# Attention on one Trainium2 core: the row maxima moved from PSUM to SBUF, and two PSUM banks given to the common ring

## The chip, the core and the metric

The kernel runs as one program on one core of a Trainium2 chip. A core has five engines with queues of their own that work side by side: PE (TensorE, matrix products into PSUM), DVE (VectorE), ACT (ScalarE), POOL (GpSimd) and SP (SyncE, which here only issues DMAs). Each engine works through its own queue in order; semaphores make one wait for another. The metric is the device time of one execution in microseconds (us); lower is better.

## The reference

Three layers on one sequence of 512 tokens of 512 features, all in fp32: a cross attention to 8192 context tokens, a linear-attention stack of eight layers, and a small expert layer. Only the first is touched by the change. Cut to what matters:

```python
xn = layer_norm(x, gamma_x, beta_x)            # the context, 8192 tokens
ln = layer_norm(latents, gamma_l, beta_l)      # the 512 tokens
q = (ln @ Wq)                                  # 8 heads of 64
k_x, v_x = halves of xn @ Wkv;  k_x = rope_rotate_k(k_x)
k_l, v_l = halves of ln @ Wkv
k, v = concat of the context's and the tokens' own
sim = einsum('bhid,bhjd->bhij', q * d ** -0.5, k)
attn = softmax(sim, axis=-1)
out = einsum('bhij,bhjd->bhid', attn, v) @ Wo
```

There are 8192 + 512 = 8704 keys, that is 68 chunks of 128 keys.

## The kernel before, in words

The eight heads are taken as four pairs. A pair's 68 chunks are cut into units of at most 13 chunks; there are 24 units and 4 x 68 = 272 chunks of a pair of heads in all. The attention runs in steps of two chunks, 136 steps, and each step also carries a piece of the work that makes keys and values of a later block of the context (`keys_of`, `values_of`, L290 and L308) and of its normalization (L179, L92 to L104, L218).

For every chunk, PE multiplies keys by queries into two PSUM banks `pc`, one for each head, 128 keys by 512 queries (`score`, L477). ACT copies each into half of an SBUF tile `sc` of 128 x 1024 (L480), and DVE keeps a running elementwise maximum `mx` of the unit (L484, L486). At the end of a unit `maxima` transposes `mx` on PE (L495), reduces it on DVE to one maximum for each query (L498 to L501) and makes the factor `alpha` by which the earlier sums of this pair are shrunk (L504: two small SBUF tiles subtracted, 128 x 8). Then `maxima_rows` spreads the maxima over all partitions with eight PE transposes into `mbc` (L513), two PSUM banks wide, 128 x 1024.

`exponentials` works on the chunks of the unit while the next unit's scores are made: DVE subtracts `mbc` from `sc` in place (L541, one instruction for a chunk and both heads), ACT takes the exponential in place (L542), and POOL adds the tile into the unit's sum `es` (L550 for the first, L552 for the others; all of its operands lie in SBUF). `weigh` (L562) then multiplies it by the values on PE, and `sums` (L601) adds up `es` over the keys.

PE's queue is in the order in which the program is written (`manual_schedule`); the queues of DVE, ACT, POOL and SP are ordered by the framework's scheduler, with some hints (`issue_after`). POOL's queue in this part also holds the rotation of the keys (L315, L316), their DMAs to DRAM (L319), the scaling of the normalized features (L218) and small steps of the reciprocal roots (L92 to L104).

PSUM has eight banks. Here `ps_s`, a ring of five, serves `pc`, `pk`, `pv`, the transposes of `maxima` and others; `ps_m` holds one tile of two banks, first `means` (the column means of the weights, used once near 100 us by `column_means` and `centre_weights`), then every unit's `mbc`; `ps_o` holds one bank for the weighted values. The tiles `sc` come from `sp`, a ring of 19.

Of the kernel before, what the change touches and what calls it, by code (L numbers as in the profile page):

```python
# [8 lines left out]
F32 = mybir.dt.float32  # L9
I32 = mybir.dt.int32  # L10
AF = mybir.ActivationFunctionType
ALU = mybir.AluOpType
AX = mybir.AxisListType
PSUM = bass.MemoryType.PSUM
# [3 lines left out]
P = 128  # L18
D = 512
DC = D // P  # L20
T = 512
TT = T // P
# [17 lines left out]
C_GX, C_BX, C_GL, C_BL = 0, 4, 8, 12  # L40
# [15 lines left out]
def perceiver_kernel(  # L56
# [3 lines left out]
    nc = tc.nc  # L60

    def pool(name, bufs, space=None, stack=ctx, **kw):
        if space is not None:
            kw["space"] = space
        return stack.enter_context(tc.tile_pool(name=name, bufs=bufs, **kw))
# [9 lines left out]
    ident = cpool.tile([P, P], F32, name="ident")  # L75
    make_identity(nc, ident)
    x_sb = res.tile([P, TT, D], F32, name="x_sb")
    col = cpool.tile([P, NCOL], F32, name="col")
# [50 lines left out]
    def weights(p, src, name, queue=nc.sync):  # L129

        w = big_tile(p, name)[:, : DC * 512].rearrange("p (c f) -> p c f", c=DC)
        queue.dma_start(out=w, in_=src.rearrange("(c p) f -> p c f", p=P))
        return w


    xa = ExitStack()
# [4 lines left out]
    xpool = pool("xattn", 1, stack=xa)  # L141
    kvp = pool("x_kv", 16, stack=xa)
    ktp = pool("x_k", 4, stack=xa)
    sp = pool("x_s", 19, stack=xa)
    dram = pool("x_dram", 1, DRAM, stack=xa)
    ps_s = pool("ps_s", 5, PSUM, stack=xa)
    ps_m = pool("ps_m", 1, PSUM, stack=xa)
    ps_o = pool("ps_o", 1, PSUM, stack=xa)
    xa.enter_context(tc.manual_schedule(engines={nc.tensor.engine}))

# [6 lines left out]
    def bank(name, shape=None):  # L157
        return ps_s.tile(shape or [P, BLK], F32, tag="s", name=name)
# [71 lines left out]
    wkv = wpool.tile([P, 2, DC, D], F32, tag="wkv", name="wkv")  # L230
# [11 lines left out]
    g_d = xpool.tile([P, DC], F32, name="g_d")  # L242
# [26 lines left out]
    def column_means(i):  # L269

        for dc in range(DC):
            nc.tensor.matmul(
                means[:, i, :], g_d[:, dc : dc + 1].to_broadcast([P, P]), wkv[:, i, dc, :],
                start=(dc == 0), stop=(dc == DC - 1),
            )

    def centre_weights(i):

        for dc in range(DC):
            w = wkv[:, i, dc, :]  # L280
            nc.vector.scalar_tensor_tensor(
                w, w, col[:, C_GX + dc : C_GX + dc + 1], means[:, i, :], ALU.mult, ALU.subtract
            )

    def projected(ps, lhs, rhs):
# [10 lines left out]
    def keys_of(b, j):  # L296

        pk = bank("pk")
        projected(pk, lambda dc: wkv[:, 0, dc, j * P : (j + 1) * P], lambda dc: xT[b, dc])
        half = j % 2  # L300
        if half == 0:
            for c in ("cos0", "sin0", "sin1", "cos1"):
                part[c] = tmp.tile([P, BLK], F32, tag=c, name=c)
        if b == 0:
            nc.scalar.copy(part["cos" + str(half)], pk)
        else:
            for i, c in enumerate(("cos", "sin")):
                nc.vector.scalar_tensor_tensor(  # L308
                    part[c + str(half)], pk, bias[:, 0, j : j + 1], trigs[b][:, i, :], ALU.add, ALU.mult
                )  # L310
        if half == 0:
            return
        lo, hi = part["cos0"], part["cos1"]
        if b:
            nc.gpsimd.tensor_tensor(lo, lo, part["sin1"], ALU.subtract)  # L315
            nc.gpsimd.tensor_tensor(hi, hi, part["sin0"], ALU.add)  # L316
        k_dr[b, j // 2] = dram.tile([2, P, BLK], F32, name=f"k{b}_{j // 2}")
        for i, half_of in enumerate((lo, hi)):
            (nc.gpsimd if b > 1 else nc.sync).dma_start(out=k_dr[b, j // 2][i], in_=half_of)  # L319
# [98 lines left out]
    normalize_block(2)  # L418
    for j in range(DC):
        keys_of(0, j)  # L420
    means = ps_m.tile([P, 2, T], F32, tag="m", name="means")
    column_means(0)
    centre_weights(0)
    column_means(1)
    for j in range(DC):
        beta_of(1, j)
        values_of(0, j)
    centre_weights(1)


# [38 lines left out]
    scores, mx, mrow, alpha, mbc, es, po = {}, {}, {}, {}, {}, {}, {}  # L469
# [36 lines left out]

    def maxima_rows(u):

        mbc[u] = ps_m.tile([P, 2, T], F32, tag="m", name="mbc")
        m = mrow[units[u][0]]  # L510
        for c in range(2 * TT):
            h, qc = divmod(c, TT)
            nc.tensor.transpose(  # L513
                mbc[u][:, h, qc * P : (qc + 1) * P], m[:, c : c + 1].to_broadcast([P, P]), ident
            )

    def factor(u):

# [117 lines left out]
    for u, n in enumerate(size):  # L636
        at(end[u], maxima if end[u] in pieced else late_maxima, u)
        at(end[u] + 1, maxima_rows, u)
        if units[u][1]:
            at(end[u] + 1, factor, u)  # L640
            at(end[u] + (3 if n > 11 else 2), shrink, u)
        for b in range(units[u][1] // TT, (units[u][2] - 1) // TT + 1):
            c0, c1 = max(units[u][1], b * TT), min(units[u][2], (b + 1) * TT)
            at(
                max(-1, (end[u] * 2 + 1 - n + c0 - units[u][1]) // 2 - 2),
                load_keys, u, b, (c0 - b * TT) * P, (c1 - b * TT) * P,
            )
        span = size[u + 1] if u + 1 < len(size) else n
        first = last + 1 if u + 2 < len(size) else 0
        for i in range(n):  # L650
            d = end[u] + 1 + i * span // n // 2
            at(d, late_exponentials if d in end[-3:] else exponentials, u, i)
            last = max(d + 1, first)
            at(last, late_weigh if u == len(size) - 2 and last == end[-1] else weigh, u, i)
        at(last, sums, u)
        if u == last_of[units[u][0]] and u + 1 < len(size):
            at(last + 1, sums_by_query, u)
            at(last + 2, ones_over, u)

    rank = {maxima_rows: 0, factor: 3.5, maxima: 2, exponentials: 3, shrink: 4, ones_over: 4, weigh: 5, sums: 6, late_weigh: 6.5, late_maxima: 7, late_exponentials: 8}  # L660
    for d in range(min(todo), max(todo) + 1):
        behind[1] = behind[0]
        for s in steps[2 * d : 2 * d + 2] if d >= 0 else ():
            score(*s)
        whole = {maxima, maxima_rows, sums_by_query}
        halved[0] = not any(f in whole for f, a in todo.get(d, []))
        for f, a in sorted(todo.get(d, []), key=lambda e: rank.get(e[0], 1)):
            f(*a)
# [44 lines left out]
    with ExitStack() as s_:  # L713
# [608 lines left out]
        for o in (4, 5):  # L1322
            w = cpl.tile([P, DC, D], F32, tag=("curT", "cur")[o % 2], name=f"f2_{o}")
# [86 lines left out]
        for o in range(NO + 2):  # L1410
            if o < NO:
                inner(o)
            if o < 2:
                w = weights(big, f2[(6 + o) * 512 : (7 + o) * 512, :], f"f2_{6 + o}", nc.scalar)
# [79 lines left out]
```

## Time and profile before

| | |
|---|---|
| median of 3 runs | 2559.41 us (2559.37 to 2564.78) |
| the profiled execution's own time | 2560.21 us |
| its span, first to last instruction | 2558.4 us |
| share of the span: PE, DVE, POOL, ACT | 97%, 70%, 53%, 44% |
| attention steps, about 115 to 1185 us: busy PE, DVE, POOL, ACT | 1040.0, 824.2, 798.6, 605.0 us of 1070 |
| L541, `sc` minus `mbc`, 272 times | 318.8 us of DVE |
| L550 and L552, `es` sums, 23 and 222 times | 54.5 and 526.3 us of POOL |
| mean granted TensorE clock | 0.993 |

How to read it: the profile is of one execution. A row of a group gives the line of the kernel, the engine, the operation, what it writes and reads, shapes, count, then busy time in us and the mean of one in ns, then the idle time of the engine ahead of it and what ended that. An instruction's duration on DVE and POOL includes time in which it has begun and is held up by something that the rows do not name. The idle time of an engine that others do not wait for costs nothing.

### The profile page before, as it was taken

How to read it: one execution, taken by the hardware profiler on the slowest of the kernel's cores; microseconds unless marked ns; L12 is line 12 of the kernel's file. 1: busy time of each engine (PE TensorE's matmuls, PEld its weight loads, DVE VectorE, ACT ScalarE, POOL GpSimd, SP SyncE). 2: the span in 40 equal slices, each digit the busy share in tenths (PEclk: the TensorE clock that was granted, in tenths of full speed). 3: DMA queues.
4: the chain of work that ended last, by engine and by line, in shares of the span. 5: the costliest groups of instructions: out<-in, count | busy, mean ns of one | idle time of the engine just before them, and what ended most of it. 6: DMA issues, size and time to landing. Idle time of an engine off the chain costs nothing.

```text
span 2558.4 us, 33959 instructions
## 1 busy us (share of the span) xinstructions
PE 2493.9 (97%) x11712; PEld 1465.9 (57%) x11712; DVE 1783.0 (70%) x3722; ACT 1128.1 (44%) x2180; POOL 1364.9 (53%) x1496
## 2 busy tenths in 40 slices
PE   8999999999999999987999999999999999999998
PEld 4433333333333333333688686877868778687763
DVE  4467778777786777886765757667576676766764
ACT  2255555555555555663434415244152531525303
POOL 1157777777777876873153442535426353273512
PEclk9999999999999999998999999999999999999999
DMA  4222222222222221011523232232322323222235
GB/s 168 68 80 78 68 81 72 72 75 71 76 75 71 77 73 45 31 33 42 188 92 95 82 99 96 75 107 75 106 84 74 112 70 111 79 75 99 71 119 191
DMA packets 110019, 221.04 MB, mean 86 GB/s; under 512 B 7640, under 2 KB 11352, under 8 KB 109848
## 3 DMA queue, kind: packets, MB, share of 16 engines
q1 hardware_dynamic: 95336, 185.11, 21.6%
q10 hardware_dynamic: 8688, 15.94, 2.1%
q0 software_dynamic: 5824, 17.83, 1.9%
q8 instruction: 93, 1.52, 0.2%
q14 instruction: 78, 0.64, 0.1%
HBM read 195.78 MB, written 18.87 MB: 84 GB/s over the span
## 4 chain that ended last, share of the span: by engine, by line
PE 86%; DVE 6%; issue 2%; ACT 2%; POOL 2%; DMA 1%; ACTq 0%; DVEq 0%; POOLq 0%
PE pb L958 14%; PE ps L747 12%; PE pw L842 9%; PE pv L290 8%; PE pc L477 8%; PE pk L290 8%; PE po L562 7%; PE ps L842 6%; PE po L1121 4%; DVE sc L541 2%; POOL es L552 1%; PE pf L1051 1%; PE pt L1040 1%; PE mbc L513 1%; PE pmx L495 1%
## 5 line engine op out<-in xcount | busy, mean ns | idle before, releaser
L552 POOL TENSOR_TENSOR es<-es,sc 128x1024 f32<-128x1024 f32 x222 | 526.3, 2371 | 60.1 <-ACT sc L542 42.7
L542 ACT ACTIVATE sc<-sc 128x1024 f32<-128x1024 f32 x272 | 288.3, 1064 | 280.4 <-DVE sc L541 267.5
L486 DVE TENSOR_TENSOR mx<-pc,mx 128x512 f32<-128x512 f32 x448 | 281.5, 682 | 162.0 <-ACT sc L480 161.8
L480 ACT COPY sc<-pc 128x512 f32<-128x512 f32 x544 | 282.5, 599 | 92.6 <-PE pc L477 86.8
L541 DVE TENSOR_TENSOR sc<-sc,mbc 128x1024 f32<-128x1024 f32 x272 | 318.8, 1206 | 4.3 <-PE mbc L513 4.3
L477 PE MATMUL pc<-qT,kt 64*128 64x512 f32 x1088 | 283.6, 617 | 2.8 <-DVE sin L308 2.2
L562 PE MATMUL po<-sc,v 128*64 128x512 f32 x1088 | 262.8, 603 | 0.0
L290 PE MATMUL pk<-xn,wkv 128*64 128x512 f32 (+1 forms) x792 | 220.8, 603 | 5.0 <-DVE sin L308 2.6
L290 PE MATMUL pv<-wkv,xn 128*64 128x512 f32 (+1 forms) x816 | 220.8, 603 | 4.7 <-DVE sin L308 2.6
L477 PEld LDWEIGHTS pc<-qT,kt 64*128 64x128 f32 x1088 | 100.4, 186 | 181.2 <-issue 94.0
L1131 ACT ACTIVATE h<-h,col 128x256 f32<-128x256 f32 x192 | 103.7, 575 | 220.7 <-DVE h L891 151.1
L1015 ACT ACTIVATE g<-g 128x512 f32<-128x512 f32 x64 | 39.8, 628 | 345.5 <-DVE g L975 218.8
L842 PE MATMUL pw<-curT,cur 128*128 128x256 f32 (+1 forms) x896 | 177.2, 350 | 0.1
L924 POOL TENSOR_TENSOR sh<-h 128x128 f32<-128x128 f32 x120 | 80.8, 673 | 177.1 <-PE pb L958 172.0
L1098 POOL TENSOR_TENSOR y<-qf,y 128x512 f32<-128x512 f32 x32 | 44.5, 1390 | 244.7 <-DVE y L1097 232.1
L975 DVE TENSOR_TENSOR g<-g,pb 128x256 f32<-128x256 f32 x135 | 49.9, 416 | 158.7 <-PE pb L958 158.2
L842 PEld LDWEIGHTS pw<-curT,cur 128*128 128x128 f32 x896 | 150.2, 190 | 16.8 <-DVE curT L835 0.2
L829 POOL TENSOR_TENSOR cur<-w 128x256 f32<-128x256 f32 x128 | 93.2, 738 | 119.4 <-DVE g L1016 75.3
L290 PEld LDWEIGHTS pk<-xn,wkv 128*64 128x64 f32 (+1 forms) x792 | 72.5, 149 | 141.4 <-issue 111.2
L290 PEld LDWEIGHTS pv<-wkv,xn 128*64 128x64 f32 (+1 forms) x816 | 71.4, 147 | 142.4 <-issue 105.3
L562 PEld LDWEIGHTS po<-sc,v 128*64 128x64 f32 x1088 | 74.5, 138 | 133.5 <-issue 124.3
L958 PE MATMUL pb<-tw,sh 128*128 128x256 f32 x540 | 136.2, 379 | 0.0
(240 smaller groups left out, 4777.8 us busy)
## 6 DMA issues: line engine op xcount, KB each, us to landing
w<-in_wf SPq DMA_DIRECT2D x64, 1024.0 KB
cb<-in_cx SPq DMA_DIRECT2D x62, 256.0 KB
xn<-in_cxt SPq DMA_DIRECT2D x15, 1024.0 KB
k<-cos POOLq DMA_DIRECT2D x60, 256.0 KB, 2.6
kt<-k SPq DMA_DIRECT2D x108, 128.0 KB
row<-in_rows ACTq DMA_DIRECT2D x48, 256.0 KB
f<-in_f SPq DMA_DIRECT2D x10, 1024.0 KB
tg<-in_trig SPq DMA_DIRECT2D x16, 512.0 KB
```

Of the source, the lines that this page charges most:

```text
L290: nc.tensor.matmul(ps[o : o + n, :], lhs(dc)[:, o : o + n], rhs(dc), start=(dc == 0), stop=(dc == DC - 1))
L477: nc.tensor.matmul(pc[h], kt[u, b][hs, o : o + P], qT[hs, p, :], start=True, stop=True)
L480: copied[0] = nc.scalar.copy(sc[:, h, :], pc[h])
L486: behind[0] = nc.vector.tensor_tensor(mx[u][:, h, :], pc[h], mx[u][:, h, :], ALU.max)
L541: nc.vector.tensor_tensor(sc, sc, mbc[u], ALU.subtract)
L542: nc.scalar.activation(sc, sc, AF.Exp)
L552: summed[0] = nc.gpsimd.tensor_tensor(es[u], es[u], sc, ALU.add)
L562: nc.tensor.matmul(po[u][h * HD : (h + 1) * HD, :], v_sb[b, p][:, t * P + h * HD : t * P + (h + 1) * HD], scores[u, i][:, h, :], start=(i ...
L747: nc.tensor.matmul(ps[:, t0 : t0 + n], w[:, dc, c0 : c0 + P], xT[:, dc, t0 : t0 + n], start=(dc == 0), stop=(dc == DC - 1),)
L842: nc.tensor.matmul(ps, lhs[:, k], rhs[:, k], start=(k == 0), stop=(k == 1))
L958: nc.tensor.matmul(ps[i], lhs, rhs, start=(q == 0 and i in (1, 2, 6, 5, 4)), stop=(q == self.N - 1 and i in (1, 2, 7, 3, 4)),)
L1131: nc.scalar.activation(h, h, AF.Gelu_apprx_tanh, bias=col[:, c : c + 1])
```

## The change

`mbc` becomes an SBUF tile of 128 x 1024 from `xpool`, one buffer. In `maxima_rows` the eight transposes go, four for each head, into a bank `pm` of the common ring, and ACT copies each bank into its half of `mbc`. L541 is the same instruction, but reads its second operand from SBUF. The pool `ps_m` is gone, and the ring `ps_s` has seven banks instead of five; `means` becomes two banks of that ring. The ring `sp` of score tiles has 18 tiles instead of 19, which frees the room for `mbc`.

```diff
-    sp = pool("x_s", 19, stack=xa)
+    sp = pool("x_s", 18, stack=xa)
...
-    ps_s = pool("ps_s", 5, PSUM, stack=xa)
-    ps_m = pool("ps_m", 1, PSUM, stack=xa)
+    ps_s = pool("ps_s", 7, PSUM, stack=xa)
...
-                means[:, i, :], g_d[:, dc : dc + 1].to_broadcast([P, P]), wkv[:, i, dc, :],
+                means[i], g_d[:, dc : dc + 1].to_broadcast([P, P]), wkv[:, i, dc, :],
...
-                w, w, col[:, C_GX + dc : C_GX + dc + 1], means[:, i, :], ALU.mult, ALU.subtract
+                w, w, col[:, C_GX + dc : C_GX + dc + 1], means[i], ALU.mult, ALU.subtract
...
-    means = ps_m.tile([P, 2, T], F32, tag="m", name="means")
+    means = [bank("means") for i in range(2)]
...
-        mbc[u] = ps_m.tile([P, 2, T], F32, tag="m", name="mbc")
+        mbc[u] = xpool.tile([P, 2, T], F32, tag="mbc", name="mbc")
         m = mrow[units[u][0]]
-        for c in range(2 * TT):
-            h, qc = divmod(c, TT)
-            nc.tensor.transpose(
-                mbc[u][:, h, qc * P : (qc + 1) * P], m[:, c : c + 1].to_broadcast([P, P]), ident
-            )
+        for h in range(2):
+            pm = bank("pm")
+            for qc in range(TT):
+                c = h * TT + qc
+                nc.tensor.transpose(
+                    pm[:, qc * P : (qc + 1) * P], m[:, c : c + 1].to_broadcast([P, P]), ident
+                )
+            nc.scalar.copy(mbc[u][:, h, :], pm)
```

## The prediction

> **What bounds the kernel now.** The page comes first: who is busy, and where the time of the engines goes.
>
> ```profile
> PE 2493.9 (97%) x11712; PEld 1465.9 (57%) x11712; DVE 1783.0 (70%) x3722; ACT 1128.1 (44%) x2180; POOL 1364.9 (53%) x1496
> ...
> L552 POOL TENSOR_TENSOR es<-es,sc 128x1024 f32<-128x1024 f32 x222 | 526.3, 2371 | 60.1 <-ACT sc L542 42.7
> L542 ACT ACTIVATE sc<-sc 128x1024 f32<-128x1024 f32 x272 | 288.3, 1064 | 280.4 <-DVE sc L541 267.5
> ...
> L541 DVE TENSOR_TENSOR sc<-sc,mbc 128x1024 f32<-128x1024 f32 x272 | 318.8, 1206 | 4.3 <-PE mbc L513 4.3
> ```
>
> PE is the bound, and DVE's subtraction L541 has half of POOL's duration per tile. The whole-span shares hide the stage that is changed, so the next view cuts out the attention steps.
>
> ```profile
> 115.00:300.00 185.00, 180.58 (x795) 68.63 (x794) 132.23 (x185) 102.78 (x195) 124.45 (x115) 0.99 0.24 77
> ...
> 700.00:900.00 200.00, 195.88 (x909) 72.92 (x906) 153.90 (x217) 111.36 (x204) 155.62 (x128) 0.99 0.22 73
> ...
> 1100.00:1185.00 85.00, 69.00 (x344) 29.25 (x340) 71.10 (x93) 51.31 (x80) 64.24 (x27) 0.92 0.06 17
> sum 1070.00, PE 1040.01 PEld 394.85 DVE 824.23 ACT 604.99 POOL 798.63; mean PE 173.33 PEld 65.81 DVE 137.37 ACT 100.83 POOL 133.10
> ```
>
> The columns after the length are PE, PEld, DVE, ACT and POOL. In these 1070 us PE idles for 30, DVE for 246, POOL for 271. So at most 30 us can be won here while PE's work stays the same, and DVE and POOL, each near 75%, are close behind. The waits of PE say what a larger ring could win:
>
> ```profile
> PE mbc L513 <- DVE sc L541: 10.9, 3, 4.9
> ...
> PE means L272 <- DVE wkv L281: 2.8, 1, 2.8
> PE pk L290 <- DVE sin L308: 2.6, 1, 2.6
> ```
>
> PE waits 10.9 us for the old `mbc` to come free, with 7.9 more put down to its weight loads; the waits for a ring bank are 2 to 3 us each.
>
> The deciding view is another: what happens to a DVE instruction whose two inputs both lie in SBUF while POOL works. L541 is none now (its `mbc` is in PSUM), but L504 is one, on 8 elements, and L218 another.
>
> ```profile
> L541 DVE TENSOR_TENSOR sc<-sc,mbc x272: 1168/1210/1221, 120.3 to 1183.5; 128x1024 f32<-128x1024 f32 x136
> L504 DVE TENSOR_TENSOR alpha<-mrow x20: 159/468/4189, 267.3 to 1175.4; 128x8 f32<-128x8 f32 x20
> L218 POOL TENSOR_TENSOR xn<-xn,rbc x58: 1256/1277/1768, 64.5 to 997.4; 128x512 f32<-128x512 f32 x58
> ...
> L218 DVE TENSOR_TENSOR xn<-xn,rbc x2: 692/1224/1755, 64.5 to 65.1; 128x512 f32<-128x512 f32 x2
> ```
>
> In minimum/median/maximum, L541 hardly varies. L504 goes from 159 to 4189 ns for the same 8 elements. The timeline of both engines at two of those says why (start, length):
>
> ```profile
> 421.95 2.09 DVE L504 TENSOR_TENSOR alpha<-mrow 128x8 f32<-128x8 f32 x1
> 738.01 1.72 DVE L504 TENSOR_TENSOR alpha<-mrow 128x8 f32<-128x8 f32 x1
> ```
>
> ```profile
> 421.68 2.34 POOL L552 TENSOR_TENSOR es<-es,sc 128x1024 f32<-128x1024 f32 x1 [1.77 <-ACT sc L542]
> 737.36 2.35 POOL L552 TENSOR_TENSOR es<-es,sc 128x1024 f32<-128x1024 f32 x1
> ```
>
> POOL's instructions end at 424.02 and 739.71, DVE's at 424.04 and 739.73: DVE stood until POOL was through. It goes the other way too: where DVE and POOL both run L218 at 64.5 us, POOL's took 1768 ns instead of 1277 and DVE's second 1755 instead of 692. Neither slows the other in part; they exclude each other. After the change L541 is of this kind, 272 times.
>
> **The change part by part.** The queues of the two kernels, compared by name: PE's instructions keep their order, DVE and POOL keep theirs with a few places swapped, ACT gets 48 copies, SP swaps one fetch of features with two of rows (loads that are issued blocks ahead: 0).
>
> *Exclusion, seen from the pair of engines.* POOL's 798.6 us and L541's 318.8 us (the same windows for L541 alone) may not overlap: 1117.4 us. Of POOL's, 60 DMA issues L319 at 567 ns, 34 us, may not take part; without them 1083. The floor is so 13 to 47 us above 1070, with neither engine ever idle. POOL idles 271 us now, mostly for things that an in-order queue goes on waiting for (`pd`, keys, exponentials). I take half to stay, 136: 1083 + 136 = 1219, or +149.
>
> *Exclusion, seen from DVE.* DVE's rows in order give 155 runs of adjacent L541 (70 single, 61 double, the rest longer), so 155 firsts and 117 followers. A first meets POOL at a random point: L504's sum, 15.3 us, less 20 x 0.16 is 0.61 us of waiting each; 155 x 0.61 = 95. A follower meets a POOL instruction that was held up by the one before it and has just begun, as the second L218 did. POOL's large ones (245 of 2.37, 58 of 1.29, 60 of 1.28) have a mean of 2.0; 117 x 2.0 = 234. DVE then needs 824 + 95 + 234 = 1153. Of its 246 idle, 162 are waits for score copies that PE paces, and go when DVE is late; I leave 60: 1213, or +143. The bounds of the waits are 0 and 272 x 2.37 (each meets a whole `es` sum) = 645 us: at the one end the other account alone decides, at the other DVE needs 824 + 645 = 1469, +399. I take the two accounts' middle, +146.
>
> *How this reaches PE:* a late L541 makes ACT's exponential late (267.5 us of ACT's idle is already this wait), then `weigh`, which PE meets in its fixed order; and behind L541 in DVE's queue stand L486 and L308, which free ring banks. Seven banks instead of five let PE run ahead by one more chunk, which evens out single delays but can't repay 146 us of demand.
>
> *L541's own time.* With both operands in SBUF and nobody in the way, DVE's row of 128x512 takes 692 ns (L1016), with one in PSUM 690 (L1014): 0. [...]
>
> *Who is let in first.* L504 at 267.31 took 4.19 us, over a POOL row of L315 and two of L218 and the DMA issue between; in the other cases DVE got in after one. [...]
>
> *48 copies on ACT* (2 x 24 units) by L480's 599 ns: 28.8 us, on 605 of 1070, so beside other work. They lengthen the path from `mrow` to the first L541 by 1.2 us a unit; DVE has L484 and L486 of the next unit meanwhile (it stood for `mbc` twice, 4.3 us). 0, at most 29 if that cover is gone.
>
> *`mbc`'s single buffer.* PE's wait of 10.9 + 7.9 us becomes a wait of ACT's copy for the last L541 of the unit before; behind it in ACT's queue stand the score copies and exponentials, and for those DVE's L486. A swap: between -19 and +19, taken at 0. *Ring of five to seven:* at most PE's other idle, 11 us; 0 while DVE is late. *`means` in two banks:* at most the 2.8 us above, 0.
>
> *18 score tiles.* Counted in PE's order, no chunk of the 272 took a tile ahead of its `weigh` with 19, seven do with 18. The nearest row is ACT's copy waiting for L552, 2.3 us in two times: 7 x 1.2 = 8 us of ACT, which idles for 465: 0; at worst a whole step of 7.8 us each, 55.
>
> Sum: 2560.2 (the profiled execution, span 2558.4) + 146 = 2706; the median is 0.8 lower: 2705.
>
> **The rivals.**
> *DVE keeps its turn* in a run: followers wait for nothing. DVE needs 824 + 95 + 60, below 1070, and POOL sets the end: 1083 to 1117 and some 30 idle, +43 to +77, about 2620. For it: in the L504 rows DVE mostly got in at the first gap. Against: the second L218.
> *DVE is passed over or always meets a full sum*: 272 x 2.0 = 544, 824 + 544 = 1368, +298, about 2858. For it: the row of 4.19 us. Against: it is one of 20.
> *Faster, by `mbc` freed from PE's queue*: if L541 excludes POOL only briefly, so that DVE's waits stay under its 246 us of idle (0.9 us each) and POOL's delays under its 271, PE loses the 18.8 us of waits: 2541. Against: L218 shows whole lengths, and the sum of 1083 is over 1070 already.
> *No change*: as PE's order is the same, the two more banks do nothing, and the waits just fit. 2560.
>
> **How the numbers follow.** The forecast 0.60, own range +85 to +230 (2645 to 2790: DVE's idle left between 0 and its half, followers meeting 1.3 to 2.4 us); DVE keeps its turn 0.22; passed over 0.12; faster 0.04; the same 0.02. A measurement of this kernel can tell 0.2%, 5 us, from no change. The range goes from 2605 (below it only part of the second case and the last two) to 2850 (above it half of the third). Slower 0.94, same 0.02, faster 0.04.
>
> **What would show it.** In the changed profile L541's minimum stays near 1.2 us while its mean goes to 2 us or more with a maximum of 3.5 and up; some L552 take over 3 us; PE's waits for L541, L542 or DVE's bank releases grow from 30 to over 150 us in this stage, which ends near 1330; after it nothing changes. If L541's mean stays at 1.21 the exclusion is wrong; if L552's mean grows by 1.2 and L541's hardly does, DVE keeps its turn.

## The result

The changed kernel takes 2701.44 us (median of 5 runs, 2695.06 to 2703.44) against 2559.41 of the kernel before (5 runs beside it, 2559.09 to 2564.78): 1.0547 times as long, 95% interval 1.0532 to 1.0562. The forecast was 2705.

In the changed kernel's profile the lines have moved a little: the subtraction is L543 (before L541), the exponential L544, POOL's sums L552 and L554 (before L550 and L552), the running maximum L485, the maxima's transposes L494, the spreading of them L514, ACT's new copy L517. From its page, engines and costliest groups (count, then busy us, mean ns, idle time ahead):

```profile
PE 2556.8 (95%) x11712; PEld 1477.9 (55%) x11712; DVE 2004.8 (74%) x3722; ACT 1145.7 (42%) x2228; POOL 1487.3 (55%) x1496
...
L554 POOL TENSOR_TENSOR es<-es,sc 128x1024 f32<-128x1024 f32 x222 | 593.2, 2672 | 102.7 <-ACT sc L544 87.5
L543 DVE TENSOR_TENSOR sc<-sc,mbc 128x1024 f32<-128x1024 f32 x272 | 536.7, 2007 | 4.6 <-ACT mbc L517 3.5
L544 ACT ACTIVATE sc<-sc 128x1024 f32<-128x1024 f32 x272 | 287.4, 1060 | 483.1 <-DVE sc L543 470.8
```

The same 272 subtractions take 2007 ns in the mean instead of 1206, POOL's same sums 2672 instead of 2371. ACT's wait for the subtraction goes from 267.5 to 470.8 us. The spread (minimum, median and maximum in ns) says that the subtraction did not become slower by itself:

```profile
L543 DVE TENSOR_TENSOR sc<-sc,mbc x272: 1174/1226/9781, 117.3 to 1332.5; 128x1024 f32<-128x1024 f32 x136
```

Minimum and median are within 16 ns of those of before (1168 and 1210); the mean is made by a part of them, up to 9.8 us: 130 of the 272 take over 1.3 us. One that took 5.90 us, with POOL at that time (start, length; two views):

```profile
648.44 5.90 DVE L543 TENSOR_TENSOR sc<-sc,mbc 128x1024 f32<-128x1024 f32 x1
```

```profile
648.44 2.51 POOL L217 TENSOR_TENSOR xn<-xn,rbc 128x512 f32<-128x512 f32 x2
650.88 5.67 POOL L554 TENSOR_TENSOR es<-es,sc 128x1024 f32<-128x1024 f32 x2
```

DVE began at 648.44 and ended at 654.34. POOL did two scalings and one sum, to about 653.2 (an undisturbed sum takes 2.36), and only then did DVE's work come, to end 1.1 us later; the second sum of the row then stood for DVE, and so two sums need 5.67 us. The stage as a whole, first the changed kernel, then the one before (length, then PE, PEld, DVE, ACT, POOL, granted clock, DMA):

```profile
117.00:1334.00 1217.00, 1104.36 (x4770) 407.38 (x4770) 1042.84 (x1152) 619.81 (x1133) 918.61 (x618) 0.95 0.17 57
```

```profile
120.00:1185.00 1065.00, 1035.54 (x4747) 392.43 (x4747) 819.96 (x1149) 602.74 (x1086) 795.63 (x617) 0.99 0.20 65
```

From the first subtraction to the end of the last, the stage grew from 1064.4 to 1216.4 us, 152 us; it began 3 us earlier and what comes after it is some 6 us shorter. PE now idles 113 us of it instead of 30, and its busy time grew by 69 us for nearly the same matmuls (4770 in the one window, 4747 in the other), while the granted clock fell from 0.99 to 0.95. Where PE stands now (waits in us in total, times, longest):

```profile
PE pmx L494 <- DVE mx L485: 42.6, 14, 6.4
PE pc L476 <- DVE mx L485: 21.5, 18, 2.8
PE pd L603 <- POOL es L554: 15.3, 3, 6.7
...
PE po L564 <- ACT sc L544: 5.9, 7, 2.0
```

The old waits for `mbc` are gone; at the end of a unit PE stands for DVE's last maximum, and in the last units for POOL's sums. For late exponentials, at the weighing (L564), it stands only 5.9 us: the delay reaches PE through the maxima that stand behind the subtractions in DVE's queue, and hardly through ACT.

### The profile page after: what moved, and what is told of

It reads as the page before. It is cut to its first block, busy times and chain, and to the rows that moved or that the text cites. A ratio compares the mean times of both kernels' runs of the same rounds, so it can differ in the third digit from the quotient of the medians.

```text
span 2701.7 us, 33993 instructions
## 1 busy us (share of the span) xinstructions
PE 2556.8 (95%) x11712; PEld 1477.9 (55%) x11712; DVE 2004.8 (74%) x3722; ACT 1145.7 (42%) x2228; POOL 1487.3 (55%) x1496
## 4 chain that ended last, share of the span: by engine, by line
PE 66%; DVE 19%; issue 8%; ACT 5%; POOL 1%; DMA 1%; ACTq 0%; DVEq 0%; POOLq 0%; SPq 0%
PE pb L960 13%; DVE sc L543 13%; PE ps L749 13%; PE pw L844 8%; PE ps L844 6%; PE pk L289 4%; PE pc L476 4%; PE pv L289 3%; PE po L1123 3%; PE po L564 3%; DVE mx L485 2%; ACT sc L479 2%; PE pf L1053 1%; ACT sc L544 1%; PE pt L1042 1%
## 5 line engine op out<-in xcount | busy, mean ns | idle before, releaser
L554 POOL TENSOR_TENSOR es<-es,sc 128x1024 f32<-128x1024 f32 x222 | 593.2, 2672 | 102.7 <-ACT sc L544 87.5
L543 DVE TENSOR_TENSOR sc<-sc,mbc 128x1024 f32<-128x1024 f32 x272 | 536.7, 2007 | 4.6 <-ACT mbc L517 3.5
L544 ACT ACTIVATE sc<-sc 128x1024 f32<-128x1024 f32 x272 | 287.4, 1060 | 483.1 <-DVE sc L543 470.8
L485 DVE TENSOR_TENSOR mx<-pc,mx 128x512 f32<-128x512 f32 x448 | 282.9, 683 | 100.7 <-ACT sc L479 100.5
L476 PE MATMUL pc<-qT,kt 64*128 64x512 f32 x1088 | 309.9, 633 | 37.4 <-DVE mx L485 21.5
L564 PE MATMUL po<-sc,v 128*64 128x512 f32 x1088 | 276.1, 628 | 7.2 <-ACT sc L544 5.9
L476 PEld LDWEIGHTS pc<-qT,kt 64*128 64x128 f32 x1088 | 105.9, 189 | 237.0 <-issue 129.5
L289 PE MATMUL pv<-wkv,xn 128*64 128x512 f32 (+1 forms) x816 | 228.4, 618 | 0.3 <-DVE sin L307 0.3
L289 PE MATMUL pk<-xn,wkv 128*64 128x512 f32 (+1 forms) x792 | 226.7, 614 | 0.0
L564 PEld LDWEIGHTS po<-sc,v 128*64 128x64 f32 x1088 | 75.6, 143 | 151.8 <-issue 121.4
L289 PEld LDWEIGHTS pv<-wkv,xn 128*64 128x64 f32 (+1 forms) x816 | 73.5, 151 | 146.4 <-issue 118.4
L289 PEld LDWEIGHTS pk<-xn,wkv 128*64 128x64 f32 (+1 forms) x792 | 73.8, 152 | 141.0 <-issue 112.4
```

The lines of the kernel that those rows point to most:

```text
L289: nc.tensor.matmul(ps[o : o + n, :], lhs(dc)[:, o : o + n], rhs(dc), start=(dc == 0), stop=(dc == DC - 1))
L476: nc.tensor.matmul(pc[h], kt[u, b][hs, o : o + P], qT[hs, p, :], start=True, stop=True)
L485: behind[0] = nc.vector.tensor_tensor(mx[u][:, h, :], pc[h], mx[u][:, h, :], ALU.max)
L543: nc.vector.tensor_tensor(sc, sc, mbc[u], ALU.subtract)
L544: nc.scalar.activation(sc, sc, AF.Exp)
L554: summed[0] = nc.gpsimd.tensor_tensor(es[u], es[u], sc, ALU.add)
```

## The experiments

**One part alone: the SBUF operand.** The kernel before, with only this:

```diff
+        pm = ps_m.tile([P, 2, T], F32, tag="m", name="pm")
+        mbc[u] = xpool.tile([P, 2, T], F32, tag="mbc", name="mbc")
...
+        for h in range(2):
+            nc.scalar.copy(mbc[u][:, h, :], pm[:, h, :])
```

and 18 score tiles; the ring keeps five banks.

> One part alone: L541 reads its maxima from SBUF, but the common ring stays at five banks and the spread maxima keep the two banks of ps_m. Exclusion theory (DVE with two SBUF inputs and POOL take turns): 2670 to 2730 us, about the changed kernel's 2701; L541 keeps its minimum near 1.17 us and has a mean of 1.9 to 2.1. Rival (the loss comes from the other queue orders, the ring or the waits for the single mbc): within 10 us of 2560, and L541 at 1.21 throughout.

2739.06 us, ratio 1.0697 (1.0680 to 1.0714): the loss is there without the larger ring, and 9 us above the range expected. The subtraction (L544 here) has a minimum of 1175 ns, a mean of 1.94 us and a maximum of 9752 ns.

**The other parts alone: copies and score ring.** ACT copies the spread maxima to SBUF, 18 score tiles, and the subtraction goes on reading PSUM:

```diff
+        spare_rows = xpool.tile([P, 2, T], F32, tag="mbc", name="unread")
+        for h in range(2):
+            nc.scalar.copy(spare_rows[:, h, :], mbc[u][:, h, :])
```

> The 48 ACT copies are made and the score ring has 18 tiles, but L541 goes on reading PSUM and nothing reads the copies. Exclusion theory: 2555 to 2575 us, L541 at 1.21 with a maximum below 1.3. Rival (copies on ACT or the lost score tile cost): 2600 us or more, with waits of ACT's copies and of L486.

2557.15 us, ratio 0.9993 (0.9983 to 1.0002): no difference that can be told.

```profile
L544 DVE TENSOR_TENSOR sc<-sc,mbc x272: 1170/1212/1223, 120.4 to 1182.8; 128x1024 f32<-128x1024 f32 x136
```

The same copies, the same ring of tiles, an operand in PSUM: no subtraction takes over 1223 ns. So the operand carries the loss, and the copies and the lost score tile none that can be told.

**Ring of five in the changed kernel** (`pool("ps_s", 5, PSUM)`).

> The changed kernel with five banks in the ring instead of seven, two banks unused. Exclusion theory: the two banks soften single delays, so it is 2700 to 2740 us. Rival (the larger ring itself brings PE into trouble): it falls towards 2560. Second rival (the two banks carry most of the load): 2760 or more.

2724.43 us, ratio 1.0640 (1.0624 to 1.0656). The two more banks are worth 23 us against the changed kernel's 2701.44: they help, and the loss is not theirs.

**Without POOL's sums,** in both kernels, and with every second one in the changed kernel:

```diff
-        elif i:
-            summed[0] = nc.gpsimd.tensor_tensor(es[u], es[u], sc, ALU.add)
```

```diff
-        elif i:
+        elif i % 2:
```

> The changed kernel without POOL's 222 sums of L554 (the denominators are left incomplete). Exclusion theory: POOL hardly competes, so L543 falls to a mean of 1.25 to 1.45 us and the time to within 25 us of the kernel before with the same sums left out, near 2560. Rival (the loss is not POOL's doing): it stays 100 us or more above that one.

> The control: the kernel before without POOL's 222 sums of L552 (the denominators are left incomplete). Both theories: PE is the bound and was hardly waiting for POOL, so 2540 to 2562 us.

> The changed kernel with every second sum of L554 left out (incomplete denominators). Exclusion theory: the wait of L543 falls with POOL's presence, mean 1.5 to 1.7 us, and the time to 2590 to 2640. Rival (no matter how much POOL works): 2690 or more.

Without the sums: 2538.56 us in the changed kernel (ratio to the kernel before 0.9916, 0.9901 to 0.9931) and 2551.77 in the control (0.9964, 0.9951 to 0.9977). The 142 us turn into a gain of 13.

```profile
L543 DVE TENSOR_TENSOR sc<-sc,mbc x272: 1170/1216/7471, 114.8 to 1166.9; 128x1024 f32<-128x1024 f32 x136
```

The subtraction's mean is 1.42 us, not quite 1.21, because POOL still scales features, rotates keys and makes the first sum of each unit (L552): 24 of 272 wait more than 0.3 us, 56 us together. So it took POOL's sums to make the loss, and the other parts of the change (seven banks, no wait of PE for `mbc`) together are worth 13 us without them, net of these waits; which of the parts, no run separates.

With 102 sums of 222 it is 2575.80 us (1.0063, 1.0048 to 1.0078), below the range expected: the mean is 1.56 us, so 95 us of waiting against 217, but the time is only 16 us above the kernel before. DVE's idle time between the first and the last subtraction shows where the waits went: 245 us in the kernel before, 173 with half of the sums, 174 with all. The first 70 us or so of waiting went into idle time; from half of the sums to all of them the waits grew by 122 us and the stage by 127 (1089.5 to 1216.4), and the idle time gave nothing more. As far as these three points tell, the loss sets in when some 70 of the 245 us are used up, not when all are.

**PE's place at the unit's end.** The changed kernel with `at(end[u], late_maxima, u)` for every unit:

> The changed kernel with the transposes of the unit's maxima always at the end of a step in PE's order (late_maxima for every unit), so that PE first does the weighing of that step and then stands at the transposes for DVE. If PE's standing there for a late DVE (42.6 us at these transposes) and the slower clock that follows it carry much of the loss: 2640 to 2680, with fewer half-clock stretches. If DVE's waits are the whole of it and PE only follows: 2690 to 2715.

2698.56 us, ratio 1.0531 (1.0511 to 1.0550): the changed kernel's own within the intervals. PE's wait at these transposes fell from 42.6 to 19.2 us and came back in part elsewhere (at L514, 8.6 to 14.8); PE's idle time in the stage went only from 113 to 101 us, and the half-clock stretches were not fewer (26 against 21). PE follows; where it stands made no difference that can be told.

**Keeping PE at work while it stands.** Four matmuls more ahead of each unit's maxima transposes:

```diff
+        warm = bank("warm")
+        for i in range(4):
+            nc.tensor.matmul(warm, ident, wkv[:, 0, i, :], start=True, stop=True)
```

> The changed kernel with four more matmuls (128x128 by 512 columns, into a bank that nobody reads) ahead of each unit's maxima transposes, where PE stands for DVE, so that PE stays in work there; 96 in all, about 50 to 100 us of PE. If the half-clock stretches after PE's standing cost the time that PE's longer busy time suggests (some 50 us): 2640 to 2690 with fewer than half as many half-clock stretches. If they are a symptom, because DVE and POOL set the pace: 2690 to 2715 with fewer stretches. If PE's standing is no spare time: 2720 or more.

2727.24 us, ratio 1.0644 (1.0630 to 1.0659), 26 us more than the changed kernel. PE's idle time in the stage fell from 113 to 70 us and the half-clock stretches from 21 (126 us) to 14 (85 us), yet it is slower, as in the third case expected: the added matmuls were not free. What the slower clock costs by itself can't be told from this.

**The SBUF operand where POOL has least to do.** The kernel before, with only the last unit, or the last two, taking `mbc` from SBUF:

```diff
+        if u in (len(size) - 1,):
+            mbc[u] = wkv[:, 0, 0:2, :]
+            for h in range(2):
+                pm = bank("pm")
...
+                nc.scalar.copy(mbc[u][:, h, :], pm)
+            return
```

> The kernel before, with only the last of the 24 units taking its maxima by an ACT copy from SBUF (into a part of the weights' tile that is no longer read, through the ring of five). In that unit POOL makes no sums, and PE no longer waits 4.7 us for the old maxima to be released near the end of the attention. Exclusion theory: 1 to 4 us faster, 2555 to 2558, L541 of that unit at 1.2 except beside the last sums of the unit before. Rival (any SBUF operand costs): slower by 1 us or more.

> The same for the last two units. POOL still makes sums for the last but one, so its 7 subtractions exclude them: gain of the earlier release (4.9 us) against up to 7 waits of 0.8 us and later sums. Exclusion theory: between 3 us faster and 4 us slower than the kernel before, and not faster than the variant with one unit by more than 2 us. Rival (the release alone matters): 4 to 8 us faster.

2565.07 us, ratio 1.0014 (1.0005 to 1.0022), and 2571.16 us, 1.0038 (1.0024 to 1.0052). That is 3.8 and 9.9 us more than the kernel before beside them (2561.31): both expectations were missed, a gain of 1 to 4 us and at most 4 us lost. The view of the last unit's first two subtractions (L552 in this kernel; the ones that read `wkv`), and POOL:

```profile
1180.38 6.08 DVE L552 TENSOR_TENSOR sc<-sc,wkv 128x1024 f32<-128x1024 f32 x2
```

```profile
1179.71 8.94 POOL L563 TENSOR_TENSOR es<-es,sc 128x1024 f32<-128x1024 f32 x3 [4.97 <-ACT alpha L531]
```

The last unit makes no sums on POOL, but POOL is still at those of the unit before. Two subtractions take 6.08 us, three sums 8.94 instead of 7.1, and PE stands 7.9 us for sums in two waits (1.9 in one before). No version faster than the kernel before came out of these runs that also computes the sums.

**The two engines by themselves.** A small program: DVE subtracts tiles of 128x1024, POOL adds or fills tiles, 24 instructions each in a stage; in the second form both start within 2 us of each other in all stages but the one with a constant (4 us).

> A small program of its own that computes nothing of the reference: stages of 24 DVE instructions (128x1024 fp32) and 24 POOL instructions, alone and side by side. Exclusion theory: DVE at 1.17 to 1.21 us alone, with an operand in PSUM also beside POOL; with two SBUF operands beside POOL's sums (128x1024) the two alternate, DVE at a spacing of 3.5 us or, where POOL's next sum doesn't depend on the one before, passed over for several of POOL's instructions. Beside POOL memsets, which read nothing, or with one SBUF operand and a constant, it is open: 0.6 to 1.2 us if not excluded, 2 to 3.5 if it is. Rival (no exclusion, some shared rate): all durations stretched by a common factor below 1.5.

> The small program again, with DVE and POOL starting together in the stages where they did not. Beside POOL instructions that don't depend on one another (128x512): if an independent chain keeps its turn, DVE's first subtraction takes as long as the whole chain, near 29 us, and the others 1.2. If DVE gets in after one or two: durations of 2 to 4 us throughout. Beside memsets: 1.2 us if only POOL's reading excludes DVE's second input, 1.7 us or more if any POOL instruction does.

From the second form, minimum/median/maximum in ns. Beside POOL's sums of 128x1024, both operands in SBUF:

```profile
L74 DVE TENSOR_TENSOR dm<-dm,other x24: 1226/3355/3380, 424.7 to 498.0; 128x1024 f32<-128x1024 f32 x24
L75 POOL TENSOR_TENSOR es<-es,g x24: 2445/3201/3205, 425.7 to 500.3; 128x1024 f32<-128x1024 f32 x24
```

Beside POOL's independent adds of 128x512:

```profile
L78 DVE TENSOR_TENSOR dm<-dm,other x24: 1226/2277/2292, 539.3 to 588.8; 128x1024 f32<-128x1024 f32 x24
L79 POOL TENSOR_TENSOR many<-many,other x24: 2237/2237/2303, 539.3 to 590.0; 128x512 f32<-128x512 f32 x24
```

Beside memsets, and then DVE's `tensor_scalar` with a constant beside sums:

```profile
L90 DVE TENSOR_TENSOR dm<-dm,other x24: 1215/1218/1226, 821.5 to 847.7; 128x1024 f32<-128x1024 f32 x24
L91 POOL MEMSET g<- x24: 951/951/952, 822.5 to 843.2; 128x1024 f32 x24
L86 DVE TENSOR_SCALAR dm<-dm x24: 682/684/693, 713.5 to 727.4; 128x1024 f32<-128x1024 f32 x24
L87 POOL TENSOR_TENSOR es<-es,g x24: 2337/2337/12834, 717.4 to 783.5; 128x1024 f32<-128x1024 f32 x24
```

With one operand in PSUM, in the first form, DVE beside the same sums took 1214 ns and POOL 2343, where they take 1216 and 2337 alone: no effect that can be told. With two in SBUF they took strict turns, one of each in 3.24 us (77.9 us for 24 of POOL's), a little under the 2.41 + 1.14 that they take one after another alone. The rival of a shared rate, one factor below 1.5 for both, is out: beside the sums DVE's rows grow from 1218 to 3355 ns (2.75 times), POOL's from 2337 to 3201 (1.37 times). Beside memsets, which read no tile, the subtractions stayed at 1218 (1219 alone, first form). One expectation failed in this form: independent adds did not pass DVE over; they alternated as well, at 2.2 us. In the first form DVE came 26 us after such a chain had begun, and then its first subtraction took 4307 ns and waited for the last three adds of the chain, one of them already under way. So DVE was passed over there, but what decides it stays open.

## Why the prediction came out right

**The deciding view was the right one.** That L541 would join L504 and L218 as an instruction that excludes POOL is shown by the three experiments on the operand, by the pair without sums, and by the small program. The marks named beforehand: minimum 1.17 us, mean 2.01, maximum 9.8; 77 of 222 sums over 3 us; the stage ends at 1333.6 us (1330 forecast). PE's idle time grew to 113 us, not over 150: the rest of PE's delay is a longer busy time.

**DVE's account was right in the sum and wrong in its terms.** It was 824 + 95 + 234 of waits + 60 idle = 1213; measured, from the first to the last subtraction, 1216. Of the 272 subtractions 130 waited.

- *Followers* were to wait 2.0 us each, 234 us. Of 114, only 45 waited, 1.76 us in the mean: 79 us. The second L218 (1755 ns instead of 692) and the subtractions of the small program (one of each in 3.24 us) show a pending POOL getting the turn; the failing step is that POOL would always be pending. A likely reason, argued and not tested, is that the first subtraction of a run had made the exponentials late that POOL's sums need (idle of L554 for ACT: 42.7 to 87.5 us).
- *Firsts* were to wait 0.61 us; the 158 there are now waited 0.87 in the mean (85 of them 1.61, the others not), 137 us instead of 95. All waits are 217 us, where 329 were forecast.
- *Idle left to DVE* was set at 60 us; it is 174 (1217 less 1042.8). The waits for score copies that PE paces were to go; before and after, they are:

```profile
DVE mx L486 <- ACT sc L480: 161.8, 106, 3.9
```

```profile
DVE mx L485 <- ACT sc L479: 100.5, 102, 2.9
```

The terms missed by 112 and by 114 us, with opposite signs: the total of this account was luck to that extent.

**POOL's account came out, with smaller misses.** It was 1083 us of work that excludes each other and 136 with neither at it, 1219. In the trace a subtraction or an instruction of POOL other than a DMA issue is under way, waiting counted in, for 1051 of the 1216 us, and neither for 165. That the work needs less than its sum fits the small program, where a pair takes 3.24 us and not 3.55. The 60 DMA issues, which the account left out, take 34.0 us in both kernels: they were not held up. That they hold up no subtraction, as 1083 instead of 1117 has it, no run shows: of the seven subtractions that began during one, two took 1216 and 1226 ns, and five took 2.4 to 4.0 us and ended 1.1 us after the sum or the rotation that came next on POOL.

**The range.** +85 to +230 does not follow from the two bounds that it names: by DVE's account, 0 to 123 us of idle time left and followers at 1.3 to 2.4 us give +1 to +253.

**Taken at nothing.** The copies and the 18 score tiles: rightly, 0.9993. The ring: wrongly, "0 while DVE is late" is 23 us (2724.43 to 2701.44), and it may have a part in the 13 us of gain without sums. The operand alone with five banks costs 165 to 180 us (2724 and 2739, each against 2558.79 beside it), more than the 146 forecast; the ring's 23 us bring it back, so that the total came within 4 us of the forecast is luck here too. With five banks DVE idles 215 us of the stage and PE 142, with seven 174 and 113. PE freed from its wait for `mbc` was put at 0; it may have a part in these 13 us too.

**The way to PE.** The prediction named two: late exponentials, and the work behind the subtraction in DVE's queue. The second carried it, 42.6 and 21.5 us of PE's waits for the maxima against 5.9 for exponentials.

**Not in the prediction: PE's clock.** In the stage, the trace's record of the granted clock has 4 stretches at half speed before, 20.5 us in all, and 21 after, 126.3 us, 18 of them within 5 us of the start of a stand of PE of 1.7 to 6.7 us. Eight matmuls of the weighing (L564) take 3.68 us within one of them, at 808.86, and 1.89 us at full clock (L562 before, at 705.18). PE was busy in 109 us of these stretches, and in 19 before; half of the 90 us more is, by these two numbers, an estimated 45 of the 69 us by which it was busy longer. The 23 matmuls more in the window are an estimated 5 to 10 us (at the 0.21 and 0.43 us from one L289 to the next at full clock); the rest is not explained. The stretches are 3.4 us long or two or three times that, and the longest that PE stood in the 8 us before a stretch was over 4 us for ten of them and 1.1 to 3.1 us for the other eleven: these show no length of a stand from which a stretch begins. Whether the end would come earlier at full clock is open: the kernel with four more matmuls a unit had a mean granted clock of 0.984 instead of 0.976 and took 26 us more.

**The rivals.** DVE keeping its turn is out: 57 followers began while an instruction of POOL was under way, and 45 of them waited. Being passed over occurs: 12 of the 130 waits of L543 outlasted more than one POOL instruction. The faster case would have been true without POOL's sums, and half of them are already enough to end it.

## What to carry to other kernels

Before an operand moves from PSUM to SBUF, ask whether the DVE instruction then has two inputs in SBUF and whether POOL reads SBUF at that time (in the small program 3355 ns beside POOL's sums, 1218 beside memsets); if so, add that instruction's busy time to POOL's, and if the sum is over the stage's length (1083 to 1117 against 1070 us here), expect the stage to grow. A tiny instruction of the same kind in the old trace, with a minimum of 159 and a maximum of 4189 ns, tells this before the change is made. Small doses hide in idle time (95 us of waits cost 16), and only a part of it can hide them (some 70 of 245 us), so a test with half the load says little about the whole.

## What the runs showed that was not expected

The clock: PE was at half speed for a tenth of the stage (126 of 1216 us), and 18 of the 21 stretches began within 5 us of the start of a stand of only 1.7 to 6.7 us. DVE's `tensor_scalar` on one SBUF tile and a constant, at 684 ns for 128x1024, let POOL wait for all that was left of a series of 24 (17 more instructions) and not for one: POOL's first sum took 12834 ns and ended after DVE's last, while the subtractions with two SBUF inputs changed turns with the same sums, one of each in 3.24 us. And the variants of the last units lost 4 and 10 us where 1 to 4 of gain, or little, was expected, and POOL was still at the sums of the unit before: that a unit makes no sums does not mean that POOL is free while it runs.
